# Convolution, attention and projection over a 48x48 image: three engines in source order, other places for the norm steps

## The chip, the cores and the metric

The kernel runs on one core of a Trainium2 chip. The metric is device time in microseconds (us), of the one core that runs.

## What is computed

The input x is 4 images of 384 channels and 48x48 = 2304 tokens, all float32. Cut to what matters:

```python
local = depthwise_conv7x7(x) * inv + shift              # inv, shift: batch norm folded
x_norm = layernorm(x_flat)                              # over the 384 channels of a token
q, k, v = split(x_norm @ qkv_w.T + qkv_b)               # 8 heads of 48
q = q + layernorm(local_flat)
attn = softmax(einsum('bhnd,bhmd->bhnm', q, k) * 48**-0.5)
out = x_flat + (einsum('bhnm,bhmd->bhnd', attn, v) merged) @ proj_w.T + proj_b
```

## The kernel before

Channels lie on the partitions in 3 chunks of 128 (`CC`), tokens on the free axis. The 2304 tokens of an image are 6 groups (`NG`) of 384 (`G`, 8 image rows); there are 24 groups t (`NT`) in all. Image b has its keys and values of all 18 key blocks of 128 tokens in SBUF; each group's queries then run against them.

A group is 12 slots (`NSLOT`). In slot s, `scores(t, s)` takes one pair of heads p = s // 3 and 6 key blocks: for each block TensorE makes two score matmuls into a buffer of the PSUM ring `r` (3 buffers, L446) and ScalarE writes the exponential to a tile `pt` (L450). Nine `pt` buffers hold six blocks of one slot and three of the next, so the last three exponentials of a slot follow as `weigh()` of the slot before (L459, values times `pt`, 12 matmuls into `sums`) gives buffers back. After three slots `pair_end` copies `sums` out (L376). VectorE runs the 7x7 convolution of the next group: 49 taps times 3 chunks = 147 multiply-adds into `acc` (L203; the first tap is L199). `share` deals these 147 over the points of the program, about equally, up to slot 9 (`LN_SLOT`) of the group before.

Two layer norms go on inside a group t: that of `xn[b + 1, g]`, which is the next image's x (slots 3 and 4, `X_SLOT`), and that of `acc` of group t + 1 (slots 9 and 10). Each is a chain through three engines: VectorE adds the chunks (`chunk_sum`, L234, L235), TensorE spreads the mean over the partitions (`spread_mean`, L241, into the one buffer `m`), VectorE subtracts (`centre`, L245), ScalarE squares (L247), VectorE adds, TensorE spreads, ScalarE makes the inverse root in three steps (`inverse_root`, L254 to L256), VectorE refines it (`newton`, L260 to L262) and multiplies. Slots 0 to 2 also have a query projection each (`query_step`, L268, then ScalarE L349), slots 5 to 7 an output projection each (`output_step`, L268, then VectorE L424). All of these, and the means, use the one PSUM buffer `m`.

Ahead of the first group stands a loop over the 6 groups of image 0, with x norm and keys and values (`keys_values`, L268, ScalarE L302, VectorE L306). Between two images `keys_values` runs for 6 groups in a row.

The order of the instructions on each engine isn't the order of the source: a scheduler of the framework sets it from the dependences, for all five engines. The queues of SP (SyncE) carry the loads of x, slabs (image rows for the convolution) and residuals, the stores and the small moves. Weights come over ScalarE's queue (L142, L148, L151, L152), small tables over POOL's (L124, L126).

Of the kernel before, what the change touches and what calls it, by code (L numbers as in the profile page):

```python
# [2 lines left out]

# [21 lines left out]
X_SLOT, OUT_SLOT, LN_SLOT = 3, 5, 9  # L25
# [14 lines left out]
def unshifted_pass(  # L40
# [36 lines left out]
    ps_m = ctx.enter_context(tc.tile_pool(name="ps_m", bufs=1, space=bass.MemoryType.PSUM))  # L77

# [9 lines left out]
    def load_packed(dst, src):  # L88
        for p0, piece in segments(src):
            nc.sync.dma_start(out=dst[p0 : p0 + piece.shape[0]], in_=piece)  # L90
# [19 lines left out]
    load_slab(0, 0)  # L110

# [17 lines left out]
    load_packed(vec, table)  # L129
    load_packed(vec2, table2)  # L130
    for g in range(NG):
        load_x(0, g)
# [13 lines left out]
    for dst, src in ((w_v, qkv_wT[:, 2 * C :]), (w_o, proj_wT)):  # L146
        for p0, piece in segments(src):
            nc.scalar.dma_start(out=dst[p0 : p0 + piece.shape[0]], in_=piece)  # L148
    vb = const.tile([P, C], F32, tag="vb", name="vb")
    pb = const.tile([P, CC], F32, tag="pb", name="pb")  # L150
    nc.scalar.dma_start(out=vb, in_=v_b.to_broadcast([P, C]))  # L151
    nc.scalar.dma_start(out=pb, in_=proj_b)  # L152
# [13 lines left out]
    nc.gpsimd.tensor_scalar_add(inv, vec[:, :, T0 + 3], BN_EPS)  # L166
    nc.gpsimd.tensor_tensor(inv, inv, neg_half, ALU.pow)
    nc.vector.tensor_mul(inv, inv, vec[:, :, T0])
    nc.vector.tensor_mul(shift, vec[:, :, T0 + 2], inv)
    nc.vector.tensor_sub(shift, vec[:, :, T0 + 1], shift)  # L170
    for c in range(CC):
        nc.vector.tensor_scalar(cw[:, c, :], vec[:, c, 0:T0], inv[:, c : c + 1], None, ALU.mult)
# [6 lines left out]
    def conv_ops(t):  # L179
# [6 lines left out]
        for c in range(CC):  # L186
            img = slab[:, c, : (end - first) * W].rearrange("p (h w) -> p h w", w=W)
            a = acc[:, c, :].rearrange("p (h w) -> p h w", w=W)
            for tap in taps:
                dy, dx = tap // KS - PAD, tap % KS - PAD  # L190
                r0, r1 = max(g * RG, -dy), min((g + 1) * RG, H - dy)
                c0, c1 = max(0, -dx), min(W, W - dx)
                if r0 >= r1:
                    continue
# [13 lines left out]
    points = []  # L208
    for t in range(NT):
        if t % NG == 0 and t:  # L210
            points += [("kv", t, g) for g in range(NG)]
        points += [("slot", t, s) for s in range(NSLOT)]
    share = {pt: [] for pt in points}
    at = 0
    for t in range(1, NT):
        due = points.index(("slot", t - 1, LN_SLOT))
        n = CC * KS * KS
        for i in range(n):
            share[points[at + i * (due - at) // n]].append(t)
# [3 lines left out]
    def convolve(point, half):  # L223
        mine = share[point]
        cut = (len(mine) + 1) // 2
        for t in mine[:cut] if half == 0 else mine[cut:]:
# [17 lines left out]
    def centre(src, m):  # L244
        nc.vector.tensor_sub(src, src, over_chunks(m[:, :G]))  # L245
        sq = work.tile([P, CC, G], F32, tag="sq", name="sq", bufs=1)
# [3 lines left out]
    def inverse_root(m):  # L250
# [6 lines left out]
        return y, u  # L257
# [22 lines left out]
    def keys_values(b, g):  # L280
        src = xn[b, g]
        k = big.tile([P, CC, G], F32, tag=f"k{g}", name=f"k{b}_{g}")
        k3 = big.tile([P, G], F32, tag=f"kt{g}", name=f"kt{b}_{g}")
        v = big.tile([P, NB, NH, HA], F32, tag=f"v{g}", name=f"v{b}_{g}")
        nc.gpsimd.memset(v[:, :, :, HD:HA], 1.0)
        for u0 in range(0, CC + NB, 2):
# [12 lines left out]
            for j in range(2):  # L299
# [11 lines left out]
        gather_tails(k3, k)  # L311
        keys[b, g], values[b, g] = (k, k3), v
# [3 lines left out]
    for c in range(CC):  # L316
        st = staged[c]
        heads = st[:, :, 0:288].rearrange("p i (c h d) -> p i c h d", h=2, d=HD)
        tails = st[:, :, 288:384].rearrange("p i (h c r) -> p i h c r", h=2, r=16)
        for h in range(2):  # L320
            nc.scalar.copy(w_qk[:, c, :, :, 64 * h : 64 * h + HD], heads[:, :, :, h, :])
            nc.scalar.copy(w_qk[:, c, :, :, 64 * h + HD : 64 * h + 64], tails[:, :, h, :, :])
    for i in range(2):
        m = bank()
        for u in range(CC):
            project(m[:, u : u + 1], lambda c: w_qk[:, c, i, u, :], lambda c: beta[:, c : c + 1])
        nc.vector.tensor_add(qkb[:, i, :], m[:, 0:CC], vec2[:, :, 2 + i])

    nc.vector.tensor_add(qkb[:, 0, :], qkb[:, 0, :], beta)
    m = bank()  # L330
    project(m[:, :C], lambda c: beta[:, c : c + 1].to_broadcast([P, P]), lambda c: w_v[:, c, :])
    nc.vector.tensor_add(vb, vb, m[:, :C])
    for c in range(CC):
# [750 lines left out]
```

## Time and profile before

| | us |
|---|---|
| median of 3 runs | 3590.05 (3585.33 to 3592.63) |
| the profiled execution | 3587.64 |
| its span, first to last instruction | 3585.8 |
| TensorE busy in the span | 3128.2 |
| VectorE busy | 2296.8 |
| ScalarE busy | 1579.6 |
| mean granted TensorE clock | 0.929 of 2.4 GHz |

A timeline row has the start and the length in us, the engine, the line of the kernel, the operation with its tiles, and how many instructions were merged; in brackets stand the idle time ahead of it and what ended that. TensorE appears as PE, VectorE as DVE, ScalarE as ACT, GpSimd as POOL; a queue of an engine has a q behind its name. Each float32 matmul leaves two records, so a slot's 12 score matmuls are "x24". Lengths of neighbouring rows of one engine can overlap a little, so the rate of a row of work is best taken from start to start.

### The profile page before, as it was taken

How to read it: one execution, taken by the hardware profiler on the slowest of the kernel's cores; microseconds unless marked ns; L12 is line 12 of the kernel's file. 1: busy time of each engine (PE TensorE's matmuls, PEld its weight loads, DVE VectorE, ACT ScalarE, POOL GpSimd, SP SyncE). 2: the span in 40 equal slices, each digit the busy share in tenths (PEclk: the TensorE clock that was granted, in tenths of full speed). 3: DMA queues.
4: the chain of work that ended last, by engine and by line, in shares of the span. 5: the costliest groups of instructions: out<-in, count | busy, mean ns of one | idle time of the engine just before them, and what ended most of it. 6: DMA issues, size and time to landing. Idle time of an engine off the chain costs nothing.

```text
span 3585.8 us, 41771 instructions
## 1 busy us (share of the span) xinstructions
PE 3128.2 (87%) x15788; PEld 1400.6 (39%) x15788; DVE 2296.8 (64%) x4287; ACT 1579.6 (44%) x2275; POOL 8.5 (0%) x39
## 2 busy tenths in 40 slices
PE   3679889889899898898899989889889997988997
PEld 2334334334354333333335434334334443433443
DVE  6999685685783758757759195595595636856010
ACT  1235445445424454454442545445444353544553
POOL 0000000000000000000000000000000000000000
PEclk9789889889899998998999989889889998989998
DMA  5110101101111111111011001001101101000000
GB/s 99 24 23 16 36 18 27 39 18 29 32 26 25 26 25 29 26 27 32 20 27 37 21 17 40 23 18 37 31 11 39 19 18 30 11 17 21 15 22 28
DMA packets 78403, 96.68 MB, mean 27 GB/s; under 512 B 23728, under 2 KB 68592, under 8 KB 78192
## 3 DMA queue, kind: packets, MB, share of 16 engines
q1 hardware_dynamic: 74240, 91.27, 11.6%
q10 hardware_dynamic: 3760, 2.64, 0.4%
q8 instruction: 126, 2.06, 0.2%
q14 instruction: 85, 0.70, 0.1%
q0 software_dynamic: 192, 0.01, 0.0%
HBM read 68.50 MB, written 14.83 MB: 23 GB/s over the span
## 4 chain that ended last, share of the span: by engine, by line
PE 49%; DVE 45%; ACT 3%; issue 2%; DMA 1%; SPq 0%; DVEq 0%; ACTq 0%
DVE acc L203 38%; PE r L446 21%; PE o L459 19%; PE m L268 5%; PE m L241 2%; ACT pt L450 2%; PE r L268 1%; DVE q L357 1%; DVE v L306 1%; DVE acc L355 1%; DVE acc L199 1%; DVE xn L245 1%; DVE ao L544 1%; DVE u L260 0%; ACT ao L376 0%
## 5 line engine op out<-in xcount | busy, mean ns | idle before, releaser
L203 DVE SCALAR_TENSOR_TENSOR acc<-slab,cw,acc 128x368 f32<-128x368 f32 (+8 forms) x3456 | 1835.6, 587 | 32.4
L450 ACT ACTIVATE pt<-r 128x768 f32<-128x768 f32 x1728 | 1279.1, 811 | 960.1 <-PE o L459 593.8
L446 PE MATMUL r<-q,k 48*128 48x384 f32 x5184 | 956.5, 515 | 288.4 <-ACT pt L450 273.2
L459 PE MATMUL o<-pt,v 128*49 128x384 f32 x6912 | 1189.0, 494 | 0.0
L446 PEld LDWEIGHTS r<-q,k 48*128 48x128 f32 x5184 | 455.2, 192 | 779.9 <-ACT pt L450 504.2
L459 PEld LDWEIGHTS o<-pt,v 128*49 128x49 f32 x6912 | 430.0, 125 | 729.8 <-issue 729.8
L424 DVE SCALAR_TENSOR_TENSOR xr<-m,pb,xr 128x384 f32<-128x384 f32 x72 | 44.4, 617 | 458.3 <-PE m L268 458.3
L446 PE MATMUL r<-qt,kt 48*128 48x384 f32 x1728 | 304.5, 498 | 1.6 <-ACT pt L450 1.6
L245 DVE TENSOR_TENSOR acc<-acc,m 128x1152 f32<-128x1152 f32 x24 | 32.5, 1354 | 364.4 <-PE m L241 364.4
L268 PE MATMUL m<-ao,w_o 128*128 128x384 f32 x432 | 166.6, 524 | 57.5 <-DVE xr L424 50.5
L446 PEld LDWEIGHTS r<-qt,kt 48*128 48x128 f32 x1728 | 147.0, 185 | 158.9 <-ACT pt L450 79.1
L268 PE MATMUL r<-xn,w_qk 128*128 128x384 f32 x432 | 155.1, 516 | 25.3 <-issue 21.6
L268 PE MATMUL m<-xn,w_qk 128*128 128x384 f32 x432 | 161.5, 511 | 4.5 <-DVE u L260 2.4
L247 ACT ACTIVATE sq<-xn 128x1152 f32<-128x1152 f32 x24 | 27.9, 1164 | 294.6 <-DVE xn L245 294.6
L268 PE MATMUL r<-w_v,xn 128*128 128x384 f32 x432 | 143.2, 486 | 0.0
L302 ACT ACTIVATE k<-r,qkb 128x384 f32<-128x384 f32 x72 | 39.2, 579 | 230.7 <-PE r L268 230.7
L349 ACT ACTIVATE q<-m,qkb 128x384 f32<-128x384 f32 x72 | 42.0, 583 | 222.6 <-PE m L268 222.6
L260 DVE SCALAR_TENSOR_TENSOR u<-m,eps,u 128x384 f32<-128x384 f32 x48 | 29.5, 616 | 168.9 <-ACT u L256 168.8
L268 PEld LDWEIGHTS m<-ao,w_o 128*128 128x128 f32 x432 | 79.3, 197 | 138.2 <-DVE xr L424 55.8
L268 PEld LDWEIGHTS r<-xn,w_qk 128*128 128x128 f32 x432 | 86.8, 203 | 93.2 <-issue 38.0
L241 PE MATMUL m<-sum,mean_w 128*128 128x384 f32 x192 | 101.7, 616 | 24.0 <-DVE u L260 13.7
L268 PEld LDWEIGHTS m<-xn,w_qk 128*128 128x128 f32 x432 | 77.3, 192 | 83.9 <-issue 38.7
(62 smaller groups left out, 772.7 us busy)
## 6 DMA issues: line engine op xcount, KB each, us to landing
xr<-in_x_dram SPq DMA_DIRECT2D x24, 576.0 KB
out_dram<-xr SPq DMA_DIRECT2D x72, 192.0 KB
slab<-in_x_dram SPq DMA_DIRECT2D x32, 378.0 KB
xn<-in_x_dram SPq DMA_DIRECT2D x48, 216.0 KB
rb<-rden SPq DMA_DIRECT2D x48, 216.0 KB
slab<-in_x_dram SPq DMA_DIRECT2D x16, 297.0 KB
slab<-in_x_dram SPq DMA_DIRECT2D x32, 126.0 KB
xn<-in_x_dram SPq DMA_DIRECT2D x48, 72.0 KB
```

The lines of the kernel that those rows point to most:

```text
L199: nc.vector.tensor_scalar(dst, src, weight, shift[:, c : c + 1], ALU.mult, ALU.add)
L203: nc.vector.scalar_tensor_tensor(dst, src, weight, dst, ALU.mult, ALU.add)
L241: nc.tensor.matmul(m[:, :G], lhsT=mean_w, rhs=s, start=True, stop=True)
L245: nc.vector.tensor_sub(src, src, over_chunks(m[:, :G]))
L268: nc.tensor.matmul(dst, lhsT=weights(c), rhs=src(c), start=c == 0, stop=c == CC - 1)
L302: nc.scalar.activation(k[:, u, :], r[:, j, :G], AF.Identity, bias=qkb[:, 1, u : u + 1])
L306: nc.vector.tensor_add(v[:, u - CC, :, 0:HD], r[:, j, :C].rearrange("p (h d) -> p h d", d=HD), vb.rearrange("p (h d) -> p h d", d=HD),)
L349: nc.scalar.activation(q[:, u, :], m[:, :G], AF.Identity, bias=qkb[:, 0, u : u + 1])
L424: nc.vector.scalar_tensor_tensor(xr[:, co, :], m[:, :G], pb[:, co : co + 1], xr[:, co, :], ALU.add, ALU.add)
L446: nc.tensor.matmul(r[:, j, :G], lhsT=kk[:, blk * P : (blk + 1) * P], rhs=qq, start=True, stop=True)
L450: nc.scalar.activation(pt, r[:, :, :G], AF.Exp, scale=SCALE)
L459: nc.tensor.matmul(sums[r : r + HA, :G], lhsT=values[t // NG, kb // NB][:, kb % NB, 2 * p + j, :], rhs=pt[:, j, :], start=kb == 0, stop=kb ...
```

## The change

1. `tc.manual_schedule` for TensorE, VectorE and ScalarE: these three engines' instructions are written in the order of the source. SP and POOL are still ordered by the scheduler.
2. `conv_ops` has its loops turned: the taps are outside and the 3 chunks inside, so three neighbouring multiply-adds write three different chunks. The 147 are dealt to half slots, each with a room (`spare`) of 4.0 less what else VectorE has there.
3. The norm steps are moved apart. For x: mean in slot 4, squares at the start of slot 5, second mean and root in slot 7, `newton` at the start of slot 8. For `acc`: slots 6, 7, 9 and 10 (8, 9, 10 and 11 in group 0). Output projections stand in slots 5, 8 and 10. `divide` (L394 and its loads) moves from the end of slot 0 to the start of slot 2.
4. Values leave PSUM by a ScalarE copy; their bias no longer is added to them but goes, through `proj_wT`, into the output bias once (`output_bias`). `keys_values` is a generator of three pieces.
5. Ahead of the first group the norm of x, the pieces of `keys_values` of the group before, and 30 multiply-adds per group are written one after the other; 49 multiply-adds of group 1 are done there too. x is loaded ahead of the tables, the tables come over ScalarE's queue, the weights over POOL's.

```diff
+X_SLOTS = 4, 7
+OUT_SLOTS = 5, 8, 10
...
+    engines = {mybir.EngineType.PE, mybir.EngineType.DVE, mybir.EngineType.Activation}
+    ctx.enter_context(tc.manual_schedule(engines=engines))
...
     load_slab(0, 0)
+    for g in range(NG):
+        load_x(0, g)
...
         for p0, piece in segments(qkv_wT[:, 0 : 2 * C]):
-            nc.scalar.dma_start(
+            nc.gpsimd.dma_start(
...
-        for c in range(CC):
-            img = slab[:, c, : (end - first) * W].rearrange("p (h w) -> p h w", w=W)
-            a = acc[:, c, :].rearrange("p (h w) -> p h w", w=W)
-            for tap in taps:
...
+        for tap in taps:
...
+            for c in range(CC):
...
+    def norm_slots(t):
+        return (6, 9) if t else (8, 10)
...
+        points += [("slot", t, s, h) for s in range(NSLOT) for h in range(2)]
+        room += [spare(t, s, h) for s in range(NSLOT) for h in range(2)]
...
+        for i in range(at, due):
+            sofar += room[i]
+            upto = round(n * sofar / total)
+            share[points[i]] += [t] * (upto - done)
+            done = upto
...
-                    nc.vector.tensor_add(
-                        v[:, u - CC, :, 0:HD],
-                        r[:, j, :C].rearrange("p (h d) -> p h d", d=HD),
-                        vb.rearrange("p (h d) -> p h d", d=HD),
+                    nc.scalar.copy(
+                        v[:, u - CC, :, 0:HD], r[:, j, :C].rearrange("p (h d) -> p h d", d=HD)
                     )
...
+        m = spread_mean(chunk_sum(src))
+        next(making, None)
+        centre(src, m)
+        sq = squares(src)
+        if g == 0:
+            taps_weights()
+        convolve_first(8)
+        m = spread_mean(chunk_sum(sq))
+        next(making, None)
+        root = inverse_root(m)
+        convolve_first(8)
+        rs = newton(*root)
...
+        nc.vector.tensor_mul(src, src, over_chunks(rs))
+        convolve_first(14)
+        next(making, None)
...
             scores(t, s)
-            convolve(point, 0)
+
+            if s == 2 and t:
+                rb = divide(t - 1)
+            if s == X_SLOTS[1] + 1 and coming is not None:
+                rs = newton(*root)
+                nc.vector.tensor_mul(coming, coming, over_chunks(rs))
+            if s == second + 1 and following:
+                query_end(t + 1, newton(*root))
+            if s == X_SLOTS[0] + 1 and coming is not None:
+                sq = squares(coming)
+            if s == first + 1 and following:
+                sq = squares(accs[t + 1])
+            convolve("slot", t, s, 0)
...
+            if s in total:
+                m = spread_mean(total.pop(s))
+            elif s in OUT_SLOTS and t:
+                output_step(t - 1, OUT_SLOTS.index(s))
             if weighing[0][0] != t or s:
                 weigh()
-            convolve(point, 1)
...
+            if s == X_SLOTS[0] and coming is not None:
+                centre(coming, m)
+            if s == first and following:
+                centre(accs[t + 1], m)
+            if (s == X_SLOTS[1] and coming is not None) or (s == second and following):
+                root = inverse_root(m)
+            convolve("slot", t, s, 1)
...
```

How the order of the instructions moves, at the three places of which the prediction speaks:

ScalarE, group 1 (of 0 to 23), before: from the exponentials (`pt<-r`) of slot 2 to those behind the x norm's squares (`sq<-xn`) and the copies at a pair's end (`ao<-o`).

```order
L349 ACTIVATE q_1615<-m,qkb 128x384
L450 ACTIVATE pt<-r 128x768 x9
L247 ACTIVATE sq<-xn_1_1610 128x1152
L376 COPY ao_1837<-o 49x384 x2
L450 ACTIVATE pt<-r 128x768 x3
L254 ACTIVATE u<-m,eps 128x384
L255 ACTIVATE y<-u 128x384
L450 ACTIVATE pt<-r 128x768 x3
```

The same engine and group now, from slot 2 to slot 10.

```order
L509 ACTIVATE pt<-r 128x768 x6
L435 COPY ao_1883<-o 49x384 x2
L509 ACTIVATE pt<-r 128x768 x12
L281 ACTIVATE sq<-xn_1_1647 128x1152
L509 ACTIVATE pt<-r 128x768 x6
L435 COPY ao_1883<-o 49x384 x2
L509 ACTIVATE pt<-r 128x768 x6
L281 ACTIVATE sq<-acc_1382 128x1152
L288 ACTIVATE u<-m,eps 128x384
L289 ACTIVATE y<-u 128x384
L290 ACTIVATE u<-y 128x384
L509 ACTIVATE pt<-r 128x768 x12
```

The squares of x stood in the middle of a slot's exponentials and now stand behind those of a whole slot (slot 5); those of `acc` and the root of x follow one another behind slot 7's.

VectorE, same group, before: the last rows of the convolution's work ahead of the x norm's `centre` (L245) and the row behind it.

```order
L199 TENSOR_SCALAR acc_2196<-slab_3_1401,cw,shift 128x384
L203 SCALAR_TENSOR_TENSOR acc_2196<-slab_3_1401,cw,acc_2196 128x8x45
L203 SCALAR_TENSOR_TENSOR acc_2196<-slab_3_1401,cw,acc_2196 128x8x46
L203 SCALAR_TENSOR_TENSOR acc_2196<-slab_3_1401,cw,acc_2196 128x8x47
L203 SCALAR_TENSOR_TENSOR acc_2196<-slab_3_1401,cw,acc_2196 128x384
L203 SCALAR_TENSOR_TENSOR acc_2196<-slab_3_1401,cw,acc_2196 128x8x47
L203 SCALAR_TENSOR_TENSOR acc_2196<-slab_3_1401,cw,acc_2196 128x8x46
L203 SCALAR_TENSOR_TENSOR acc_2196<-slab_3_1401,cw,acc_2196 128x8x45 x2
L203 SCALAR_TENSOR_TENSOR acc_2196<-slab_3_1401,cw,acc_2196 128x8x46
L203 SCALAR_TENSOR_TENSOR acc_2196<-slab_3_1401,cw,acc_2196 128x8x47
L245 TENSOR_TENSOR xn_1_1610<-xn_1_1610,m 128x1152
L203 SCALAR_TENSOR_TENSOR acc_2196<-slab_3_1401,cw,acc_2196 128x384
```

Now, the same group, from the adding of x's chunks (slot 3) over `centre` (L277, slot 4) to the projection's residual (L483, slot 5).

```order
L266 TENSOR_TENSOR sum<-xn_1_1647 128x384
L267 TENSOR_TENSOR sum<-sum,xn_1_1647 128x384
L210 SCALAR_TENSOR_TENSOR acc_1382<-slab_2_648,cw,acc_1382 128x8x46
L210 SCALAR_TENSOR_TENSOR acc_1382<-slab_2_648,cw,acc_1382 128x8x45 x6
L210 SCALAR_TENSOR_TENSOR acc_1382<-slab_2_648,cw,acc_1382 128x8x46 x3
L277 TENSOR_TENSOR xn_1_1647<-xn_1_1647,m 128x1152
L210 SCALAR_TENSOR_TENSOR acc_1382<-slab_2_648,cw,acc_1382 128x8x47 x2
L622 TENSOR_TENSOR ao_1114<-ao_1114,rb 128x1152
L210 SCALAR_TENSOR_TENSOR acc_1382<-slab_2_648,cw,acc_1382 128x8x47
L210 SCALAR_TENSOR_TENSOR acc_1382<-slab_2_648,cw,acc_1382 128x384 x3
L210 SCALAR_TENSOR_TENSOR acc_1382<-slab_2_648,cw,acc_1382 128x8x47 x3
L483 SCALAR_TENSOR_TENSOR xr_1645<-m,pb,xr_1645 128x384
```

Ten multiply-adds (eight in most groups) now stand between the adding of x's chunks and `centre`, in threes of the three chunks; before, the third chunk's stood alone, one after the other.

POOL at the start of the program, before: from its last table load on.

```order
L124 DMA table_92<-in_ln_dram 128x3x1
L126 DMA table_92<-in_qk_b_dram 48x4x1 x2
L155 MEMSET neg_half 128x3
L157 MEMSET mean_w 128x128
L159 MEMSET eps 128x1
```

And now.

```order
L94 DMA w_o<-in_proj_wT_dram 48x3x384
L94 DMA w_o<-in_proj_wT_dram 16x3x384
L155 DMA vb<-in_v_b_dram 128x384
L156 DMA pb<-in_proj_b_dram 128x3
L159 MEMSET neg_half 128x3
L161 MEMSET mean_w 128x128
L163 MEMSET eps 128x1
```

All 22 weight loads (12 of `pt`, 4 of `w_v`, 4 of `w_o`, `vb`, `pb`) now stand ahead of the fill of `mean_w`, the weights of every `spread_mean`.

## Rows read from the trace of the kernel before

**Rows 1.** The page, part 1: busy us, share of the span and instructions.

```profile
PE 3128.2 (87%) x15788; PEld 1400.6 (39%) x15788; DVE 2296.8 (64%) x4287; ACT 1579.6 (44%) x2275; POOL 8.5 (0%) x39
```

**Rows 2.** Waits: engine and line, what it waited for, us in total, times, longest.

```profile
ACT sq L247 <- DVE xn L245: 294.6, 22, 17.9
...
PE r L446 <- ACT pt L450: 274.8, 17, 17.8
...
PE m L268 <- DVE xr L424: 50.5, 5, 18.4
```

**Rows 3.** Timeline of all engines, 370 to 420 us, around the first of these stops.

```profile
373.05 9.33 DVE L203 SCALAR_TENSOR_TENSOR acc<-slab,cw,acc 128x368 f32<-128x368 f32 x18
...
382.81 6.36 DVE L203 SCALAR_TENSOR_TENSOR acc<-slab,cw,acc 128x360 f32<-128x360 f32 x10
...
390.47 1.16 ACT L247 ACTIVATE sq<-xn 128x1152 f32<-128x1152 f32 x1 [17.48 <-DVE xn L245]
...
414.60 2.21 ACT L450 ACTIVATE pt<-r 128x768 f32<-128x768 f32 x3 [1.92 <-PE r L446]
```

**Rows 4.** Timeline of PE, 367 to 535 us, two stops one group apart.

```profile
393.38 4.21 PE L446 MATMUL r<-q,k 48*128 48x384 f32 x12 [17.36 <-ACT pt L450]
...
528.01 4.21 PE L446 MATMUL r<-q,k 48*128 48x384 f32 x12 [17.39 <-ACT pt L450]
```

**Rows 5.** Timeline of PE, 300 to 325 us: a short stop in group 0.

```profile
318.70 2.32 PE L446 MATMUL r<-qt,kt 48*128 48x384 f32 x12 [1.63 <-ACT pt L450]
```

**Rows 6.** Timeline of PE, 1100 to 1250 us, one whole group without a stop.

```profile
1108.68 4.21 PE L446 MATMUL r<-q,k 48*128 48x384 f32 x24
1112.81 2.20 PE L268 MATMUL m<-xn,w_qk 128*128 128x384 f32 x6
1114.95 4.08 PE L459 MATMUL o<-pt,v 128*49 128x384 f32 x24
...
1123.25 0.91 PE L241 MATMUL m<-sum,mean_w 128*128 128x384 f32 x2
...
1223.04 4.21 PE L446 MATMUL r<-q,k 48*128 48x384 f32 x24
```

**Rows 7.** Stretches: us, busy us of each engine, PEclk (granted clock), DMA share, GB/s.

```profile
393.40:397.40 4.00, 4.00 (x12) 1.84 (x12) 3.89 (x9) 1.33 (x2) 0.00 (x0) 0.50 0.00 0
...
318.70:321.00 2.30, 2.30 (x13) 0.95 (x13) 0.25 (x1) 1.35 (x2) 0.00 (x0) 1.00 1.07 155
```

**Rows 8.** Timeline of PE, 985 to 1105 us: an image's first slot.

```profile
1084.21 0.92 PE L446 MATMUL r<-q,k 48*128 48x384 f32 x4
...
1096.27 2.20 PE L268 MATMUL m<-xn,w_qk 128*128 128x384 f32 x6
```

**Rows 9.** Groups by line and form, ACT: busy us, mean ns of one, idle before.

```profile
L376 ACT COPY ao<-o 49x384 f32<-49x384 f32 x144 | 68.0, 472 | 30.7 <-PE o L459 28.9
...
L247 ACT ACTIVATE sq<-acc 128x1152 f32<-128x1152 f32 x24 | 28.1, 1173 | 6.1 <-DVE acc L245 6.1
...
L254 ACT ACTIVATE u<-m,eps 128x384 f32<-128x384 f32 x48 | 27.9, 582 | 143.7 <-PE m L241 143.7
```

**Rows 10.** Timeline of all engines, 0 to 60 us: weight loads, the fill of `mean_w`.

```profile
4.17 17.55 ACTq L142 DMA_DIRECT2D pt<-in_qkv_wT_dram  x12
...
5.35 0.22 POOL L157 MEMSET mean_w<- 128x128 f32 x1
...
35.12 0.44 ACTq L152 DMA_DIRECT2D pb<-in_proj_b_dram  x1
```

**Rows 11.** Timeline ahead of the first group: keys and values of group 3, keys of 5, first scores.

```profile
149.51 8.21 PE L268 MATMUL r<-xn,w_qk 128*128 128x384 f32 x18 [3.73 <-issue]
157.56 5.97 PE L268 MATMUL r<-w_v,xn 128*128 128x384 f32 x18
...
193.65 8.33 PE L268 MATMUL r<-xn,w_qk 128*128 128x384 f32 x18 [3.75 <-issue]
...
218.84 8.37 PE L446 MATMUL r<-q,k 48*128 48x384 f32 x48
```

More of the change, by code (lines that the diff above doesn't have):

```diff
@@ L2 @@
 from contextlib import ExitStack
+from itertools import chain
 import concourse.bass as bass
@@ L185, in conv_ops @@
         accs[t] = acc
-        for c in range(CC):
-            img = slab[:, c, : (end - first) * W].rearrange("p (h w) -> p h w", w=W)
-            a = acc[:, c, :].rearrange("p (h w) -> p h w", w=W)
-            for tap in taps:
[L190 to L194, printed above, removed]
+        for tap in taps:
+            dy, dx = tap // KS - PAD, tap % KS - PAD
+            r0, r1 = max(g * RG, -dy), min((g + 1) * RG, H - dy)
+            c0, c1 = max(0, -dx), min(W, W - dx)
+            if r0 >= r1:
+                continue
+            for c in range(CC):
+                img = slab[:, c, : (end - first) * W].rearrange("p (h w) -> p h w", w=W)
+                a = acc[:, c, :].rearrange("p (h w) -> p h w", w=W)
                 src = img[:, r0 + dy - first : r1 + dy - first, c0 + dx : c1 + dx]
@@ L204, in conv_ops, with spare @@
                 yield
-    points = []
+    def spare(t, s, half):
+        b, g = divmod(t, NG)
+        other = 0.0
+        if b + 1 < B:
+            other += {(3, 1): 1.0, (4, 1): 1.4, (5, 1): 1.0, (8, 0): 3.0}.get((s, half), 0.0)
+        if t:
+            other += {(2, 0): 0.7, (4, 1): 1.4}.get((s, half), 0.0)
+            other += 0.6 if half and s in OUT_SLOTS else 0.0
+        if t + 1 < NT:
+            first, second = norm_slots(t)
+            other += {
+                (first - 1, 1): 1.0,
+                (first, 1): 1.4,
+                (first + 1, 1): 1.0,
+                (second + 1, 0): 4.7,
+            }.get((s, half), 0.0)
+        return max(0.0, 4.0 - other)
+    def norm_slots(t):
+        return (6, 9) if t else (8, 10)
+    points, room = [], []
     for t in range(NT):
         if t % NG == 0 and t:
-            points += [("kv", t, g) for g in range(NG)]
-        points += [("slot", t, s) for s in range(NSLOT)]
+            points += [("kv", t, g, h) for g in range(NG) for h in range(2)]
+            room += [4.0] * (2 * NG)
+        points += [("slot", t, s, h) for s in range(NSLOT) for h in range(2)]
+        room += [spare(t, s, h) for s in range(NSLOT) for h in range(2)]
     share = {pt: [] for pt in points}
@@ L215, in unshifted_pass, with convolve @@
     for t in range(1, NT):
[L216 to L219, printed above, removed]
+        due = points.index(("slot", t - 1, norm_slots(t - 1)[0], 0))
+        total, n, done, sofar = sum(room[at:due]), CC * KS * KS, 0, 0.0
+        for i in range(at, due):
[3 more added lines that the diff above has]
+            done = upto
         at = due
     streams = {}
[L223 to L226, printed above, removed]
+    def convolve(*point):
+        for t in share[point]:
             if t not in streams:
@@ L256, in inverse_root @@
         nc.scalar.activation(u, y, AF.Square)
-        return y, u
+        return m, y, u
     def newton(m, y, u):
@@ L284, in keys_values @@
         v = big.tile([P, NB, NH, HA], F32, tag=f"v{g}", name=f"v{b}_{g}")
+        keys[b, g], values[b, g] = (k, k3), v
         nc.gpsimd.memset(v[:, :, :, HD:HA], 1.0)
@@ L315, in unshifted_pass @@
+            if u0 == 2:
+                gather_tails(k3, k)
+            yield
     qkb = const.tile([P, 2, CC], F32, tag="qkb", name="qkb")
[L316 to L322, printed above, removed]
@@ L338, in unshifted_pass, with output_bias @@
+    def output_bias():
+        m = bank()
+        for co in range(CC):
+            project(
+                m[:, co : co + 1],
+                lambda c: w_o[:, c, co * P : (co + 1) * P],
+                lambda c: vbp[:, c, :],
+            )
+        nc.vector.tensor_add(pb, pb, m[:, 0:CC])
     queries = {}
@@ L549, in unshifted_pass @@
+            if s == X_SLOTS[0] + 1 and coming is not None:
+                total[X_SLOTS[1]] = chunk_sum(sq)
+            if s == first + 1 and following:
+                total[second] = chunk_sum(sq)
     weigh()
```

169 lines of the change are left out of this document (82 added, 87 removed).

## The prediction

> **What bounds the kernel now.** I read the busy times first, then the waits, then the timeline around the longest wait, and at last one stretch in which nothing waits. TensorE is busy for 87% of the span and VectorE for 64% [rows 1], so TensorE is the engine to fill. The waits say why it isn't full: ScalarE's squares of the x norm waited 294.6 us for VectorE, and TensorE's scores waited 274.8 us for ScalarE's exponentials, 17 times [rows 2]. One is the cause of the other. VectorE had 28 multiply-adds of the convolution standing ahead of `centre`; when the squares began, at 390.47, ScalarE had sat in front of them for 17.48 us, with the exponentials that hold the PSUM ring behind them [rows 3]. TensorE stopped for 17.36 us and, one group later, for 17.39 [rows 4].
>
> Sixteen stops are of this kind: the 274.8 us less the one short stop of 1.63 [rows 5], 273.2 us. They are in images 0 to 2, where an x norm goes on. In image 3 the same lateness of VectorE takes another way, an output projection that waits for the buffer `m`: of 50.5 us in 5 [rows 2] two are 0.71 each in the program's tail, so the three long ones are 49.1 us.
>
> Where nothing waits, the same work takes 114.36 us per group (1108.68 to 1223.04) [rows 6]; with a stop it is 134.63 (393.38 to 528.01) [rows 4]. The difference, 20.27, is the stop of 17.39 and 2.88 more: behind the stop TensorE goes on at a granted clock of 0.50, the lower of its two levels (1.2 of 2.4 GHz), for 4 us [rows 7], so that 12 records take the 4.21 us [rows 4] that 24 take at the full level [rows 6].
>
> **The change, part by part.** The sum is made against the profiled execution, 3587.6 us; the median of the runs is 2.4 us above it.
>
> *The stops.* With the source's order, `centre` of x needs a mean at the end of slot 4's scores, and its squares stand behind all exponentials of slot 5. A slot is 4.13 us of scores, 4.0 of weighing, 2.14 for a projection and some 0.85 for a mean [rows 6]: the first and third are from start to start, the others a row's length less the 0.07 by which neighbours overlap. From slot 4's start the mean is there at 5.0 and `centre` at 6.5, if VectorE has come so far (eight multiply-adds, 4.1 us, stand ahead of it). ScalarE comes to the squares at 18.4: slot 4 of 9.0, then scores, a projection, and 3.1 for the last exponentials, which start behind the first weighing matmuls. So 12 us of spare time stand where 17 were missing. For `acc` (slots 6 and 7) the same count gives 25.7 against 36.4. In image 3 the projections have VectorE's answer in the same slot. All 19 stops go: 273.2 + 49.1 = 322.3, and 19 x 2.9 = 55 for the slow stretches behind them.
>
> VectorE must keep up for this. A multiply-add costs 9.33 / 18 = 0.518 us where chunks alternate and 6.36 / 10 = 0.636 where one chunk's follow each other [rows 3]; in threes I take 0.518, the row of the like order. With 147 of them and 19 us for the rest (two norms, a division, three residuals) a group needs 95 us, against some 116 of TensorE. `centre` was late for its place, not for its length.
>
> *Values by ScalarE.* The first slot of an image waits twice for VectorE's values and takes 12.06 us (1084.21 to 1096.27) [rows 8] where 4.13 would do. ScalarE's copy has no row; the nearest are its other reads of `m` and `o`, 0.47 to 0.58 each [rows 9], so two end 1.2 us behind the last projection and the ring has two free buffers meanwhile. That gives back 7.9 us three times, 24. Its 3.5 us per group of keys are hidden by TensorE's keys and values, two times 18 records of some 5.9 us [rows 11]; without that cover they would cost at most those 3.5, 63 in all.
>
> *New waits.* ScalarE has a gap of 1.9 us ahead of a slot's first exponential [rows 3], and the ring lets it be some 0.3 later before TensorE feels it: 2.2. Behind slot 7 stand the squares of `acc` and the root of x, 1.17 and three of 0.53 to 0.58 [rows 9], 2.8 together: 0.7 too long, in 17 groups. Behind slot 9 the root of `acc` stands behind two copies of 0.47 that can't start before the weighing ends: 0.1 + 1.0 + 1.65 = 2.7 into slot 10, where 1.3 is free: 1.4 too long, in 22 groups. Together 12 + 31 = 43. From below it is nothing, if the ring hides it. From above, such a stop also costs the clock: 39 x 2.9 = 113 more. The row of a like stop, 1.63 us, shows the 12 records behind it in 2.32 us [rows 5] at a granted clock of 1.00 [rows 7], so I leave that out. The Trainium skill says otherwise (TensorE: Matmul & The Clock Gate, "A second HAM failure mode: psum-queue depth-cycling"): a kernel that idles shortly between groups of matmuls while it cycles through PSUM can fall back to the slow level again and again. The trace's one such stop speaks against it.
>
> The output projection of slot 8 needs `m` back from `newton` of x. By the same count ScalarE ends the root at 39.3, VectorE gives `m` back at 40 and TensorE comes at 42: 2 us to spare, the thinnest place of the group. Queues: SP's division loads now wait for slot 2 instead of slot 0's end, and x's next load stands behind them; x is needed at the end of slot 3, some 18 us later, so I cost this at nothing. Without that cover it would hold up the mean of slot 4.
>
> *The start.* Scores begin at 218.84 [rows 11]. Two things change. All weight loads go through POOL ahead of the fill of `mean_w`, which was done at 5.4 us [rows 10]; the 22 loads took ScalarE's queue from 4.17 to 35.56 [rows 10], so the first mean comes at about 39 and the convolution at 42. The bounds are no delay (it starts at about 27, when x and the tables are there) and twice the queue's time (68). Then six rounds and a last one. In a round VectorE has 30 multiply-adds (15.5) and 6.6 of norm work, about the 22.07 of a round now (44.12 us for two, 149.51 to 193.65) [rows 11]. But it now also stands still: 1 us for the mean, 1 to 3 for squares that ScalarE does behind two key copies, 2.8 for a root behind two more. I take 28 per round. 42 + 6 x 28 + 7 (layout of the weights in the first) + 26 (the last, with queries) = 243, that is 24 later. Bounds: 27 + 6 x 24 + 29 = 200, 19 earlier; 68 + 6 x 31 + 40 = 294, 75 later.
>
> By the Trainium skill (DMA: Bandwidth & Descriptors, "Anatomy of one DMA — SWDGE (gpsimd) path") a load issued from GpSimd takes about 2.0 us and its bytes at 436 GB/s. For 22 loads of 2.56 MB one after the other that is an estimate of 50 us, and the sum would be some 19 us higher; no row shows such a load of weights.
>
> *Sum.* 3587.6 - 322.3 - 55 - 24 + 43 + 24 = 3253.6. I predict **3254 us**.
>
> **The rivals.**
>
> *A slow start.* Mean weights behind POOL's queue and half-speed projections between idle rounds (8.21 us for 18 records where the next 18 take 5.97 [rows 11]) bring the upper bound: 3254 + 51 = 3305. For it: those rows. Against: VectorE's own work still covers most.
>
> *The clock falls at the short stops.* 39 x 2.9 more: 3367. Against it stands the one row above.
>
> *Stops come back at another place.* If VectorE is more than 2 us late at slot 8, the projection waits for `m` and with it everything; were half of the old 377 us paid again, the time would be 3254 + 188 = 3442. For: the three engines wait for each other in turn, and no scheduler fills a gap. Against: the 12 and 10 us at the squares.
>
> *Slower: VectorE becomes the bound.* It stops in order behind squares, roots and loads, and can't go on with the convolution. The kernel is slower when a group of 116 us costs over 14 more, so 130, in each of the 24 (334 / 24 = 14). With 19 us for the rest a multiply-add would have to cost 0.76 with all waits, against 0.518 and 0.636 [rows 3]. At 0.78 a group is 134 and the time some 3254 + 24 x 18 = 3680. Little speaks for it: VectorE has 21 us to spare per group.
>
> *The order isn't kept.* The printed order shows it kept; I give this nothing beside the cases above.
>
> **How the numbers follow.** The forecast gets 0.62, the slow start 0.18, the clock 0.08, stops elsewhere 0.07, VectorE as bound 0.04, no change of over 0.2% 0.01. A measurement of this kernel can tell 0.2%, 7 us, from nothing. The range must hold the forecast with its bounds and the slow start, 0.80: downwards the new waits may be hidden (43) and part of the start's 24 with them, so 3200; upwards the slow start's 3305 and a part of the clock, 3340. Faster 0.95, same 0.01, slower 0.04.
>
> **What would show it.** In the profile after, groups should take 115 to 118 us from slot to slot, with no stop of TensorE over 3 us behind the start; ScalarE's squares should wait for nothing and VectorE should show idle time ahead of `centre`, `newton` and the squares' sums. A multiply-add should come every 0.52 us everywhere. The short stops should stand in slots 8 and 10 alone, at the full level. The first scores should start near 243 us. I am wrong if TensorE's waits for VectorE through `m` or `sum` exceed a few us per group, if the granted clock in the main loop stays below 0.97, or if a time above 3340 comes with groups longer than 119 us.

## The result, and the profile after

| | before | after |
|---|---|---|
| median, us | 3589.61 (3585.33 to 3592.63) | 3246.46 (3243.98 to 3250.67) |
| ratio, 95% interval | | 0.9046 (0.903 to 0.9062) |
| profiled execution | 3587.64 | 3243.98 |
| its span | 3585.8 | 3241.7 |
| mean granted clock | 0.929 | 0.985 |

Predicted were 3254 us (3200 to 3340), faster. The page of the changed kernel, part 1, answers to [rows 1]:

```profile
PE 3074.7 (95%) x15806; PEld 1378.5 (43%) x15806; DVE 2207.2 (68%) x4216; ACT 1600.7 (49%) x2347; POOL 20.1 (1%) x61
```

TensorE is busy for 95% of the span instead of 87%. Its waits (us in total, times, longest) answer to [rows 2]:

```profile
DVE xr L483 <- PE m L302: 296.9, 71, 73.5
...
DVE xn L277 <- PE m L273: 251.9, 22, 67.4
...
PE m L273 <- DVE sum L267: 102.4, 15, 30.0
...
PE r L505 <- ACT pt L509: 35.4, 39, 1.3
```

The two long waits of before have turned round: `centre` (L277) now waits for its mean (longest, 67.4 us each, twice where TensorE makes the next image's keys and values), and no row has the squares waiting for it. TensorE waited 39 times for exponentials, 35.4 us in all and never over 1.35. Its 102.4 us for `sum` lie ahead of the first scores, but for 0.41. The timeline of TensorE shows where the 39 are, a group from slot 8 to slot 8; it answers to [rows 4]:

```profile
418.94 2.32 PE L505 MATMUL r<-q,k 48*128 48x384 f32 x12 [0.34 <-ACT pt L509]
439.81 2.31 PE L505 MATMUL r<-qt,kt 48*128 48x384 f32 x12 [1.35 <-ACT pt L509]
...
535.31 2.32 PE L505 MATMUL r<-q,k 48*128 48x384 f32 x12 [0.34 <-ACT pt L509]
```

That is slot 8 (17 times) and slot 10 (22 times), and the group takes 116.37 us instead of 134.63. A short stop costs more than its idle time says: in the same timeline slot 10's scores take 552.65 to 558.45, 5.80 us, slot 8's 4.79 and those of a slot without a stop 4.14.

```profile
504.42 4.21 PE L505 MATMUL r<-q,k 48*128 48x384 f32 x24
508.56 2.20 PE L302 MATMUL m<-ao,w_o 128*128 128x384 f32 x6
...
532.76 2.21 PE L505 MATMUL r<-q,k 48*128 48x384 f32 x12
535.31 2.32 PE L505 MATMUL r<-q,k 48*128 48x384 f32 x12 [0.34 <-ACT pt L509]
537.55 2.20 PE L302 MATMUL m<-ao,w_o 128*128 128x384 f32 x6
...
552.65 2.21 PE L505 MATMUL r<-qt,kt 48*128 48x384 f32 x12
556.20 2.32 PE L505 MATMUL r<-qt,kt 48*128 48x384 f32 x12 [1.35 <-ACT pt L509]
558.45 1.88 PE L302 MATMUL m<-ao,w_o 128*128 128x384 f32 x5
```

So 17 x 0.65 + 22 x 1.66 = 48 us. The other engines in the same group, VectorE first, then ScalarE:

```profile
500.52 1.35 DVE L277 TENSOR_TENSOR xn<-xn,m 128x1152 f32<-128x1152 f32 x1 [6.28 <-PE m L273]
...
534.59 0.62 DVE L294 SCALAR_TENSOR_TENSOR u<-m,eps,u 128x384 f32<-128x384 f32 x1 [0.43 <-ACT u L290]
...
513.74 1.18 ACT L281 ACTIVATE sq<-xn 128x1152 f32<-128x1152 f32 x1
```

`centre` ends at 501.87 and ScalarE comes to the squares at 513.74: 11.9 us to spare, where 17.48 were missing [rows 3] and 12 were predicted. VectorE gives `m` back at 535.2 and slot 8's projection wants it at 537.55: 2.3 us, against 2.

### The profile page after: what moved, and what is told of

It is laid out like the page before. It is cut to its first block, busy times and chain, and to the rows that moved or that the text cites. A ratio compares the mean times of both kernels' runs of the same rounds, so it can differ in the third digit from the quotient of the medians.

```text
span 3241.7 us, 41854 instructions
## 1 busy us (share of the span) xinstructions
PE 3074.7 (95%) x15806; PEld 1378.5 (43%) x15806; DVE 2207.2 (68%) x4216; ACT 1600.7 (49%) x2347; POOL 20.1 (1%) x61
## 4 chain that ended last, share of the span: by engine, by line
PE 88%; ACT 6%; DVE 3%; issue 1%; DMA 0%; SPq 0%; ACTq 0%; DVEq 0%
PE r L505 34%; PE o L518 34%; PE m L302 9%; PE r L302 9%; PE m L273 3%; DVE acc L210 2%; ACT pt L509 2%; ACT sq L281 1%; ACT u L288 1%; ACT y L289 1%; ACT u L290 1%; ACT ao L435 0%; ACT k L338 0%; DVE sum L267 0%; DVE sum L266 0%
## 5 line engine op out<-in xcount | busy, mean ns | idle before, releaser
L210 DVE SCALAR_TENSOR_TENSOR acc<-slab,cw,acc 128x376 f32<-128x376 f32 (+12 forms) x3456 | 1749.3, 583 | 0.0
L518 PE MATMUL o<-pt,v 128*49 128x384 f32 x6912 | 1173.8, 489 | 0.0
L505 PE MATMUL r<-q,k 48*128 48x384 f32 x5184 | 923.2, 501 | 6.6 <-ACT pt L509 5.8
L505 PEld LDWEIGHTS r<-q,k 48*128 48x128 f32 x5184 | 435.3, 186 | 492.7 <-ACT pt L509 252.7
L483 DVE SCALAR_TENSOR_TENSOR xr<-m,pb,xr 128x384 f32<-128x384 f32 x72 | 44.5, 618 | 296.9 <-PE m L302 296.9
L277 DVE TENSOR_TENSOR xn<-xn,m 128x1152 f32<-128x1152 f32 x24 | 32.5, 1354 | 251.9 <-PE m L273 251.9
L273 PE MATMUL m<-sum,mean_w 128*128 128x384 f32 x192 | 92.0, 562 | 102.4 <-DVE sum L267 102.4
L302 PE MATMUL r<-xn,w_qk 128*128 128x384 f32 x432 | 163.8, 537 | 0.0
L302 PEld LDWEIGHTS m<-xn,w_qk 128*128 128x128 f32 x432 | 76.2, 189 | 78.6 <-issue 27.2
L302 PEld LDWEIGHTS r<-w_v,xn 128*128 128x128 f32 x432 | 83.2, 193 | 59.0 <-issue 3.3
L266 DVE TENSOR_TENSOR sum<-sq 128x384 f32<-128x384 f32 x48 | 26.8, 558 | 115.1 <-ACT sq L281 115.1
```

The costliest lines, as they stand in the source:

```text
L210: nc.vector.scalar_tensor_tensor(dst, src, weight, dst, ALU.mult, ALU.add)
L273: nc.tensor.matmul(m[:, :G], lhsT=mean_w, rhs=s, start=True, stop=True)
L302: nc.tensor.matmul(dst, lhsT=weights(c), rhs=src(c), start=c == 0, stop=c == CC - 1)
L483: nc.vector.scalar_tensor_tensor(xr[:, co, :], m[:, :G], pb[:, co : co + 1], xr[:, co, :], ALU.add, ALU.add)
L505: nc.tensor.matmul(r[:, j, :G], lhsT=kk[:, blk * P : (blk + 1) * P], rhs=qq, start=True, stop=True)
L518: nc.tensor.matmul(sums[r : r + HA, :G], lhsT=values[t // NG, kb // NB][:, kb % NB, 2 * p + j, :], rhs=pt[:, j, :], start=kb == 0, stop=kb ...
```

## The experiments

First, one table. "First scores" is the first row of the scores in the timeline of TensorE, "the rest" is the span less that, worked out.

| kernel | median, us | first scores | the rest |
|---|---|---|---|
| before | 3590 | 218.84 | 3367.0 |
| the change | 3246.46 | 233.87 | 3007.8 |
| e1, change without source order | 3462.76 | 187.28 | 3274.8 |
| e2, before with source order | 3351.38 | 312.42 | 3037.7 |
| e8, before, order on VectorE alone | 3351.31 | 313.09 | 3035.2 |
| e9, change, order on VectorE alone | 3156.19 | 191.14 | 2963.2 |
| e3, chunk after chunk | 3278.15 | 240.56 | 3034.6 |
| e4, values by VectorE | 3263.29 | 250.74 | 3008.1 |
| e5, root in slot 10 | 3196.42 | 235.44 | 2960.4 |
| e6, start in another order | 3207.71 | 197.90 | 3008.8 |
| e7, e5 and e6 | 3154.09 | 193.51 | 2956.6 |
| e10, e7 with a new first round | 3146.58 | 185.63 | 2957.6 |

### Which engine's order it is

**e1**, the change without its first item:

```diff
-    engines = {mybir.EngineType.PE, mybir.EngineType.DVE, mybir.EngineType.Activation}
-    ctx.enter_context(tc.manual_schedule(engines=engines))
```

> The change without its first item: the framework's scheduler orders TensorE, VectorE and ScalarE again, the new places of the norm steps and everything else stay. In the printed order 34 multiply-adds then stand between x's sum and its centre, 8 with the source order. Theory (source order and places are both needed): 34 x 0.52 = 17.7 us put centre's end some 19 us behind the sum, while ScalarE comes to the squares some 12 to 18 us behind it, so stops of 1 to 7 us come back in 18 groups and, by the same lateness, at the second norm: 3270 to 3430 us. Rival (the places alone do it, the scheduler is harmless once the steps stand apart): within 20 us of the change's 3246.

3462.76 us, ratio to the kernel before 0.9652 (0.9636 to 0.9669), above the theory's range. Stops came back, of 10 to 20 us in the loop where the theory had 1 to 7. VectorE, ScalarE and TensorE at one of them (lines stand 2 lower in this kernel):

```profile
641.63 15.01 DVE L208 SCALAR_TENSOR_TENSOR acc<-slab,cw,acc 128x276 f32<-128x276 f32 x38
656.55 1.36 DVE L275 TENSOR_TENSOR xn<-xn,m 128x1152 f32<-128x1152 f32 x1
...
657.94 1.16 ACT L279 ACTIVATE sq<-xn 128x1152 f32<-128x1152 f32 x1 [11.62 <-DVE xn L275]
...
659.86 4.21 PE L503 MATMUL r<-q,k 48*128 48x384 f32 x12 [10.50 <-ACT pt L507]
```

And the row of its waits:

```profile
PE r L503 <- ACT pt L507: 231.3, 17, 20.5
```

It is the picture of [rows 3] once more: 38 multiply-adds ahead of `centre`, ScalarE in front of the squares, TensorE stopped 17 times, 15 of them behind group 0. The places alone don't do it.

**e2**, the kernel before and source order on the three engines, nothing else:

```diff
+    engines = {mybir.EngineType.PE, mybir.EngineType.DVE, mybir.EngineType.Activation}
+    ctx.enter_context(tc.manual_schedule(engines=engines))
```

> The kernel before with one line more: source order on TensorE, VectorE and ScalarE; old places of the norm steps, chunk after chunk in the convolution, values by VectorE, old start. Theory (the order alone takes the long stops away): x's squares stand behind the exponentials of slot 3, which end some 9.4 us behind the slot's start, and centre has only the 6 multiply-adds of a half slot ahead of it, so it ends at 7 to 9 us: no long stop is left. The start is written one step after the other, with 12 us of keys and values in each of six rounds on the path, so I expect first scores at 300 to 330 us, and the first slots of images keep their 8 us: 3320 to 3400 in all. Rival 1 (the places are what counts): stops of over 5 us stay in most groups, over 3450. Rival 2 (VectorE at 0.636 per multiply-add is the bound): 147 x 0.636 + 19 = 112.5 us per group leaves 2 us, and its waits push the group over 120 us: over 3450 too, but with TensorE waiting for VectorE everywhere.

3351.38 us, 0.9341 (0.9325 to 0.9356), as the theory said: between group 0, which has one of 11.01 us, and the program's tail no stop is longer than 2.58 us, though the norm steps stand in their old slots. The rows of TensorE's waits for exponentials and for the output:

```profile
PE m L271 <- DVE ao L547: 33.4, 17, 2.6
...
PE r L449 <- ACT pt L453: 10.4, 13, 2.6
```

Its rest is 329 us shorter than before's and 30 longer than the change's; its start is 94 us longer than before's. So with all three engines in source order the new places and the rest of the change gave 30 us of the loop, and repaired the start.

**e8**, the same with one engine only:

```diff
+    engines = {mybir.EngineType.DVE}
+    ctx.enter_context(tc.manual_schedule(engines=engines))
```

> The kernel before with source order on VectorE alone; TensorE and ScalarE stay with the scheduler. Theory (the long stops come from VectorE's order alone, 28 multiply-adds ahead of centre; now 6): no stop of over 5 us in the main loop, short ones of 1 to 3 us may stand where the scheduler put squares and roots between the exponentials of a slot; with a start between 219 and 312 us: 3260 to 3410. Rival (the three orders must fit each other: ScalarE's place for the squares, set by the scheduler, is what stops TensorE): stops of over 5 us stay in most groups, over 3450.

3351.31 us, 0.9338 (0.9324 to 0.9352): the time of e2. Group 0 has one stop of 13.82 us, against the expectation; behind it, up to the tail, none is over 2.58, and the waits for exponentials are short:

```profile
PE r L449 <- ACT pt L453: 8.8, 13, 0.9
```

Source order on TensorE and ScalarE adds nothing there.

**e9**, the change with source order on VectorE alone:

```diff
-    engines = {mybir.EngineType.PE, mybir.EngineType.DVE, mybir.EngineType.Activation}
+    engines = {mybir.EngineType.DVE}
```

> The change with source order on VectorE alone; TensorE and ScalarE go back to the scheduler, the places and all else stay. Theory (the scheduler does harm only where it puts multiply-adds ahead of a norm step on VectorE): none of the 17 stops of 10 to 17 us of the scheduler's version comes back; ScalarE's squares and roots may stand a few exponentials earlier or later than in the change, at up to 2 us a group: 3230 to 3300. Rival (the three orders only work together): stops of over 5 us in most groups, over 3380.

3156.19 us, 0.8792 (0.8779 to 0.8806), below the range: 90 us faster than the change. ScalarE's timeline, around the root of `acc`, shows why:

```profile
504.49 0.58 ACT L288 ACTIVATE u<-m,eps 128x384 f32<-128x384 f32 x1 [1.85 <-PE m L273]
505.10 0.52 ACT L289 ACTIVATE y<-u 128x384 f32<-128x384 f32 x1
505.53 2.19 ACT L509 ACTIVATE pt<-r 128x768 f32<-128x768 f32 x3
507.60 0.53 ACT L290 ACTIVATE u<-y 128x384 f32<-128x384 f32 x1
508.50 0.97 ACT L435 COPY ao<-o 49x384 f32<-49x384 f32 x2 [0.37 <-PE o L518]
```

And TensorE's waits have one short stop where the change has 39:

```profile
PE r L505 <- ACT pt L509: 1.2, 1, 1.2
```

The scheduler puts two of the root's three steps between a slot's third and fourth exponential, where ScalarE has time to spare (1.85 us idle), and the third behind the sixth; source order puts all three behind the sixth and behind the copies, in front of the next slot. It also orders the start better (191.14 against 233.87). Both differences, 42.7 us ahead of the first scores and 44.6 behind, make the 90 up to 3 us: on these two engines source order only cost. Which of the two engines it was, no run separates; but e7, below, reaches 3154 us with source order on all three, so the cost lies in the places that the source gives to ScalarE's extra work, and not in source order as such. And with VectorE's order alone the change's other parts are worth more than the 30 us of above: 72 us of the rest (3035.2 in e8, 2963.2 here) and 122 of the start.

### Two other parts of the change

**e3**, the convolution's loops turned back:

```diff
-        for tap in taps:
+        for c in range(CC):
...
-            for c in range(CC):
+            for tap in taps:
```

> The change with the convolution's loops turned back: one chunk's 49 taps, then the next chunk's; all else stays. Multiply-adds follow each other in one chunk and should come every 0.636 us instead of 0.52: 17 us more per group on VectorE, which is idle for about 21 us in a group of the change, and 196 x 0.118 = 23 us more ahead of the first scores. Theory (chunks in turn are needed because the idle time stands where VectorE is early and can't be used elsewhere): VectorE comes late to steps behind the longest runs of multiply-adds, stops of 1 to 6 us per group: 3290 to 3410. Rival (VectorE's spare time takes it all): only the start grows, 3246 + 23 = 3269, within 10.

3278.15 us, 0.9138 (0.9123 to 0.9153). Multiply-adds come every 0.64 us (14.03 for 22) instead of 0.517:

```profile
573.92 14.03 DVE L210 SCALAR_TENSOR_TENSOR acc<-slab,cw,acc 128x360 f32<-128x360 f32 x22
589.08 0.62 DVE L294 SCALAR_TENSOR_TENSOR u<-m,eps,u 128x384 f32<-128x384 f32 x1 [1.12 <-ACT u L290]
```

Yet from group 1's end on a group takes what it takes in the change, 116.39 us (568.90 to 685.29, slot 8 to slot 8): VectorE's spare time takes the 18 us. The 32 us were paid at the start (7) and in groups 0 and 1, where TensorE waited 9.41, 7.32 and 2.23 us for VectorE. What these waits don't make of it are slow stretches behind them (24 records in 5.83 to 6.28 us instead of 4.1). Neither theory has it whole; in the loop the rival is right.

**e4**, the values' copies by VectorE:

```diff
-                    nc.scalar.copy(
+                    nc.vector.tensor_copy(
```

> The change with the values' copies out of PSUM on VectorE instead of ScalarE; all else stays. Prediction's term: an image's first slot waits again for VectorE, 8 us three times, and rounds of the start grow by up to 2 us: 3246 + 24 to 38. Rival (in source order VectorE has 15 multiply-adds or 7.8 us and three copies or 1.9 us in 11.6 us of keys and values, so it isn't late, and the copy's engine no longer matters): within 8 us of 3246.

3263.29 us, 0.9099 (0.9084 to 0.9114). The 17 us are all in the start; the rest is that of the change within 0.3 us. An image's first slot doesn't wait in this kernel:

```profile
1012.96 4.21 PE L505 MATMUL r<-q,k 48*128 48x384 f32 x24
1017.10 2.20 PE L302 MATMUL m<-xn,w_qk 128*128 128x384 f32 x6
```

4.14 us, not 12.06 [rows 8], and the same in e2 (1100.18 to 1104.26), which has the values by VectorE as before. So VectorE's order frees the first slot without ScalarE's copies. The other way round it works too: e1, with ScalarE's copies and the scheduler's order, takes 4.14 us as well:

```profile
1063.95 4.21 PE L503 MATMUL r<-q,k 48*128 48x384 f32 x24
1068.09 2.20 PE L300 MATMUL m<-xn,w_qk 128*128 128x384 f32 x6
```

Either part is enough, and neither number of the two theories came out.

### The short stops and the start

**e5**: the squares of `acc` go to slot 8, its root behind slot 10, the last projection to slot 11 (group 0 stays, and the planner's `spare` follows).

```diff
-OUT_SLOTS = 5, 8, 10
+OUT_SLOTS = 5, 8, 11
...
-            if s == second + 1 and following:
+            if s == 11 and following:
                 query_end(t + 1, newton(*root))
...
-            if s == first + 1 and following:
+            if s == second - 1 and following:
                 sq = squares(accs[t + 1])
...
-            if (s == X_SLOTS[1] and coming is not None) or (s == second and following):
+            if (s == X_SLOTS[1] and coming is not None) or (s == 10 and following):
```

> The change with three steps of the second norm moved: the squares of acc from slot 7 to slot 8, its root from behind slot 9 (and its two copies) to behind slot 10, the third output projection from slot 10 to slot 11. Theory (the two short stops are ScalarE's extra work in front of a slot's first exponential, and each costs TensorE just its length): 17 stops of 0.34 us and 22 of 1.35 us in the profile of the change, 35.5 us, go: 3246 - 36 = 3211, group 114.5 us. Rival 1 (something else falls due at the same places, and the stops only move): over 3235. Rival 2 (the stops cost clock too): under 3195.

3196.42 us, 0.8904 (0.8892 to 0.8916): 50 us less than the change, not 36. No stop is left behind group 0, which has one of 0.40. The 50 are the 48 worked out above from the slots' lengths; my 36 had only the idle times. A group without any stop, from one second mean to the next, takes 114.05 us:

```profile
498.80 0.91 PE L273 MATMUL m<-sum,mean_w 128*128 128x384 f32 x2
...
612.85 0.91 PE L273 MATMUL m<-sum,mean_w 128*128 128x384 f32 x2
```

**e6**, the start's rounds:

```diff
         m = spread_mean(chunk_sum(src))
-        next(making, None)
         centre(src, m)
         sq = squares(src)
+        next(making, None)
...
         m = spread_mean(chunk_sum(sq))
-        next(making, None)
         root = inverse_root(m)
+        next(making, None)
```

> The change with two lines moved in the rounds ahead of the first group: the squares and the root stand ahead of the copies of keys and values of the group before on ScalarE, and so on TensorE the mean ahead of nothing new. Theory (a round of 31 us is VectorE's 24 us of work and 7 us in which it stands behind ScalarE's copies, 1.9 at the squares and 5.1 at the root): six rounds lose 6.9 us each, first scores at 234 - 41 = 193, 3246 - 41 = 3205. Rival 1 (keys and values become late instead, the ring of three buffers holds TensorE's next mean up): half or less of it, over 3225. Rival 2 (the start is hidden by nothing, but TensorE, idle less, also runs at its full level longer): under 3195.

3207.71 us, 0.8934 (0.8922 to 0.8947). First scores at 197.90, 36 us earlier, and the rest unchanged. In the change a round looked like this, ScalarE first, then VectorE:

```profile
135.25 0.58 ACT L338 ACTIVATE k<-r,qkb 128x384 f32<-128x384 f32 x1 [7.82 <-PE r L302]
135.73 0.47 ACT L342 COPY v<-r 128x384 f32<-128x384 f32 x1
136.09 0.59 ACT L288 ACTIVATE u<-m,eps 128x384 f32<-128x384 f32 x1
...
127.46 0.56 DVE L266 TENSOR_TENSOR sum<-sq 128x384 f32<-128x384 f32 x1 [1.94 <-ACT sq L281]
...
137.82 0.62 DVE L294 SCALAR_TENSOR_TENSOR u<-m,eps,u 128x384 f32<-128x384 f32 x1 [5.13 <-ACT u L290]
```

The root's mean was there at 129.6 (a record of 0.88 from 128.76), but a key and a value copy stood ahead of it, waiting for TensorE.

**e7**, both edits together:

> Both moves of the two kernels above in one. If the two costs are independent, as they lie in different stretches, the gains add: 3246 - 36 - 41 = 3169, faster than the change and than the kernel before. Rival: they share a cause (VectorE early at one place is VectorE late at the next), and less than 60 us are gained.

3154.09 us, 0.8788 (0.8776 to 0.88): 92 us, where the measured 50 and 39 add to 89 (the expected 36 and 41 to 77). The two costs are independent.

**e10**, e7 with the first round changed: fills, then x's first group, come first on POOL, and the first round's multiply-adds stand behind its norm.

```diff
+    nc.gpsimd.memset(mean_w, 1.0 / C)
...
+    load_x(0, 0, nc.gpsimd)
     load_slab(0, 0)
-    for g in range(NG):
+    for g in range(1, NG):
         load_x(0, g)
...
-        convolve_first(14)
+        if g == 0:
+            taps_weights()
+        convolve_first(14 if g else 30)
```

> The faster version (root in slot 10 and the start's copies behind squares and roots, 3154 us) with a new first round: the fills of constants and the four loads of the first 384 tokens stand first on POOL, and in the first round all multiply-adds and their weights stand behind the norm. Theory (the first sum waits 28 us for x because SP's load of x stands behind a wait for the tables, 12.2 us in the profile; it isn't the fill of mean_w, done at 26.8): the first sum starts near 10 us, the squares near 20 behind ScalarE's loads of the tables, the second round at 46 to 50 instead of 56: first scores 6 to 10 us earlier, 3144 to 3148. Rival (the weights' arrival and layout set the second round, not x): no gain, within 3 us of 3154, or a loss because the weights come later behind x.

3146.58 us, 0.8768 (0.8756 to 0.878), the fastest of all, 12.3% below the kernel before and as expected. The first sum starts at 12.84 instead of 28.39 in e7, but of these 15 us only 8 reach the first scores: the sum of the squares waits 8.83 us for ScalarE, whose loads of the tables stand ahead of the squares.

## Why the prediction was right, step by step

| term | predicted | found |
|---|---|---|
| 19 stops | -322.3 | -322.3, none left |
| slow stretches behind them | -55 | -55, not measured by itself |
| first slots of images | -24 | -24, from either of two parts |
| new waits | +43 | +48 |
| start | +24 | +15 |
| the group without a stop | 0 | -5, as worked out below |
| sum | 3253.3 | 3244 |

As written, the forecast's terms add to 3253.3 and not to its 3253.6. Behind the first scores the found terms make -358, and the rest fell by 359.2 us.

- **The stops** went for the reason given, VectorE's order: e1 brings them back, e2 and e8 take them away with nothing else changed. The clock came back with them: e1's stop of 10.50 us is followed by 12 records in 4.21 us, as in [rows 4], and the change's granted clock is 1.00 (rounded) over the stretch from 350 to 3200 us. That the *places* were needed is where my count went too far. I worked out 12 us of spare time from them; in the old places the order alone leaves no long stop behind group 0 either (e2).
- **"Source order" was taken as one thing.** The forecast took the waits it brings to ScalarE as the price of the gain. They aren't: e9 and e7 have the gain without them.
- **New waits.** Slots and counts were right, and for 38 of the 39 the level of the clock (below). The ring hid more than the 2.2 us I gave it (idle 0.34 and 1.35 where I had 0.7 and 1.4), but a stop costs 0.31 us beyond its idle time, so 43 became 48.
- **First slots.** "That gives back 7.9 us three times" came true, and ScalarE's copies can give it back (e1). They weren't needed for it: e4 shows the same gain without them, from VectorE's order. What they alone gave, 17 us, lies in the start, where I hadn't looked for it.
- **The start.** "First mean comes at about 39" was wrong, it came at 30:

```profile
5.30 1.04 POOL L146 DMA_DIRECT2D pt<-in_qkv_wT_dram  x2
...
26.58 0.22 POOL L161 MEMSET mean_w<- 128x128 f32 x1
...
28.73 0.56 DVE L266 TENSOR_TENSOR sum<-xn 128x384 f32<-128x384 f32 x1 [27.83 <-DMA xn<-in_x_dram]
...
30.03 1.62 PE L273 MATMUL m<-sum,mean_w 128*128 128x384 f32 x2 [30.03 <-DVE sum L267]
...
33.89 1.25 DVE L206 TENSOR_SCALAR acc<-slab,cw,shift 128x384 f32<-128x384 f32 x3
...
209.60 0.55 DVE L266 TENSOR_TENSOR sum<-acc 128x384 f32<-128x384 f32 x1
```

  POOL had issued its 22 loads at 26.6, before x arrived. They were issued every 0.5 to 1 us where nothing held them and landed 3.9 to 10.4 us later (medians by tile), so they overlapped. The reading of the Trainium skill's figure (DMA: Bandwidth & Descriptors, "Anatomy of one DMA — SWDGE (gpsimd) path") by which one load follows the other, an estimate of 50 us, isn't borne out. Rounds were 31 us (sums at 117.09 and 148.19), not 28: I gave the root 2.8 us behind ScalarE's copies, and it took 5.1. It was luck that this hardly shows in the sum: the first two rounds took only 27.2 and 29.9 us (sums at 28.73, 55.95 and 85.84), though the weights' layout, for which I had 7 us more, stands in the first. So from the first multiply-add to the last round's sum it was 175.7 us, where the forecast has 6 x 28 + 7 = 175. Of the 9 us by which the scores began early, 8 are the earlier first multiply-add, at 33.9 instead of 42.
- **The last 5 us**: a group without a stop takes 114.05 us (e5), 0.31 less than the row I used [rows 6]; times the 17 groups with an x norm that is the remainder. That each of them differs by as much is assumed.

Of the rivals, VectorE as the bound is far off: even at 0.64 us per multiply-add (e3) the groups keep their length. "The clock falls at the short stops" happened at one of 39, for 1.7 us. The slow start didn't come, the scores began 9 us before the forecast's 243, and no stop came back at another place.

## What to carry to other kernels

Take an engine's order away from the scheduler only where its order is what is late: here that is VectorE, where fillers were put ahead of a step on which two other engines wait, while on ScalarE and TensorE the scheduler's interleaving was worth 90 us in the changed kernel (and nothing in the old one). When a change has several parts, undo each alone before crediting one, and try each alone too: here the long stops go without the new places, and an image's first slot is freed by either of two parts. And where an engine has a gap of known length ahead of each slot, put extra work in the middle of the slot's own sequence, not at its end.

## What the runs showed of the hardware

The clock doesn't answer to every short stop. In the change 38 of the 39 (0.34 and 1.35 us) were followed by the full level. One of 1.35 us wasn't: the 12 records behind it took 2.81 us instead of 2.31, the six of the projection 3.35 instead of 2.20.

```profile
1674.17 2.81 PE L505 MATMUL r<-qt,kt 48*128 48x384 f32 x12 [1.35 <-ACT pt L509]
1676.91 3.35 PE L302 MATMUL m<-ao,w_o 128*128 128x384 f32 x6
```

Their granted clock was 0.81 and 0.64. In e3, e4 and e6, which have the same stops, it fell behind 5 of the 66 of this length and behind none of 0.34. In e2 an output projection in slot 5 waits for VectorE: behind waits of 1.15 to 1.54 us, 8 of them, the six records behind always took about 2.2 us; behind waits of 2.58 us they took 3.6 to 3.9 in 7 of 9 cases (in e8 3.2 to 3.9 in 8 of 9). Two of these, from TensorE's timeline:

```profile
495.23 2.20 PE L271 MATMUL m<-ao,w_o 128*128 128x384 f32 x6 [2.58 <-DVE ao L547]
...
612.83 3.90 PE L271 MATMUL m<-ao,w_o 128*128 128x384 f32 x6 [2.58 <-DVE ao L547]
```

And their stretches (us, busy of each engine, then the granted clock):

```profile
495.23:497.40 2.17, 2.17 (x8) 1.09 (x9) 2.06 (x4) 0.00 (x0) 0.00 (x0) 1.00 0.00 0
612.83:616.70 3.87, 3.87 (x8) 1.67 (x9) 3.66 (x7) 0.00 (x0) 0.00 (x0) 0.56 0.00 0
```

The same stop can leave the clock at 1.00 or drop it to its lower level (0.56 over the stretch). What decides between them was not tried. The section of the Trainium skill that spoke against the change (TensorE: Matmul & The Clock Gate, "A second HAM failure mode: psum-queue depth-cycling") has the clock go up and down when such a kernel idles shortly and often. This is a middle result: of 39 stops in a kernel that cycles through PSUM one cost clock, while of the somewhat longer ones, in another version of it, most did.

Multiply-adds that write the same chunk one after the other come every 0.64 us, those that alternate between three chunks every 0.517 (26.37 for 51 in the change), though one record is hardly shorter (603 ns against 610 at 376 elements): those that alternate overlap. The trace before had shown it for two chunks [rows 3].
